# Two-byte one-hot selections with the entries of a batch innermost, widened by ScalarE, in a graph transformer layer

## The chip, the cores and the metric

The kernel runs on one core of a Trainium2 chip. The metric is the device time of one execution in microseconds (us). Three runs of the kernel before took 1121.39, 1125.89 and 1126.09 us; the median is 1125.89 us. A profile of one further execution gives spans, waits and the clock granted to TensorE.

The engines are named as in the profile: PE (TensorE, matmuls) and PEld (its weight loads), DVE (VectorE), ACT (ScalarE), POOL (GpSimd), SP (SyncE, which here issues DMAs). Each runs its own instructions in order.

## The reference, cut to what matters

A layer over 3125 nodes with 256 features: layer norm; a sparse graph network (`_L0_gnn_ref`); linear attention without a softmax (`_L0_mix_ref`); then a mixture of eight experts (`_L0_ffn_ref`). There are 53,125 edges, sorted by `dst`.

```python
xn = _layernorm(x)
# graph network: row = src, col = dst, val = edge_weight
spmm = lambda v: segment_sum(val[:, None] * v[col], row, num_segments=3125)
h = spmm(xn)
s0 = softmax(spmm(h) @ W0.T + b0)
s1 = softmax(spmm(concat([s0, s0])) @ W1.T + b1)      # the four heads are equal
x = x + tanh(concat([s0, s1]) + h) + mix(xn)          # mix: q, k, v; norms of k and v; (k^T v) / n
# experts: argmax of a gate, at most 489 tokens for an expert, two layers with relu
x = x + prob * expert(layernorm(x))
```

## The kernel before

The three sparse products are computed as dense ones. In a first stage the kernel builds the adjacency matrix (transposed, 3200 x 3200, fp32) in DRAM as `adj`; then it multiplies by it three times, in seven strips of up to 512 columns (`STRIPS`). The first strip of the first product and ten chunks (of 128 rows) of the second strip are already multiplied during the building. The keys and values of the attention (`kv_tile`, L728 on) are worked in beside the rest of the first product.

**The building (`from_runs`, L405 to L655).** Edges are sorted by target, so 625 groups of five targets (`GR`) each own a short run of edges. `search` finds the start of each run, `gather` (POOL, indirect DMA) fetches 128 edges for each of 125 groups, and `turn` splits source numbers into a block (one of 25) and a cell within the block (one of 128), and turns them on TensorE so that the 128 slots of a group lie on partitions. The result is `edge`: row in the group, block, cell and weight for each slot and group, in fp32. There are five such pieces of 125 groups.

A batch is 16 groups (`GB`); there are 39 full batches and one of a single group. `batch(b)` (L557) makes two matrices for each group on DVE: `lhs` (L564), 128 slots x (5 rows x 25 blocks), the product of "which row, times weight" (`in_row`) and "which block" (`in_blk`); and `rhs` (L569), 128 slots x 128 cells, the comparison of the numbers 0 to 127 with the slot's cell. Both are fp32 and hold 16 groups. `in_row` and `in_blk` come from `selections` (L539) for three batches at a time. One matmul for each group (L578; in fp32 two weight loads and two matmul instructions) sums the slots into 125 x 128 numbers in PSUM. Four groups fill a bank, ACT copies the bank to `st_rows` (L582), and SP writes the batch to `adj` (L589, L590). The four banks are two of `acc(1)` and two of `ps_b`; `st` has two buffers, `lhs` and `rhs` three each.

**The order of the work** is written out by hand in the loop at L618; nothing is planned by a scheduler (`tc.manual_schedule`). Every third batch a step of a node strip's layer norm is set between the batches. There are three steps: `norm_a` (DVE statistics L364, ACT square root L367) ahead of batches 0, 3, 6 ...; `norm_b` (DVE L373 and L375, four ACT instructions L379, eight TensorE transposes L386) behind batches 1, 4, 7 ...; `norm_c` (two ACT copies L393 out of PSUM) ahead of batches 2, 5, 8 ... Strips 2 to 6 are done so, which takes batches 0 to 14; strips 0 and 1 come before batch 0. `turn` stands ahead of a batch whose number leaves 1 when divided by 3, where a new piece is needed. `finish` (L325) prepares the gate's weights behind batch 18: two fp32 matmuls (L329) and a DVE instruction (L332) that waits for them.

`ask` loads a finished chunk of `adj` rows (L596, SP), and `take` multiplies it (L272: four instructions for a chunk, two feature halves in fp32). Reads go into `first_a`, six buffers.

After the building the pools of that stage are closed, new ones are laid in the same memory, and the weights of keys and values (`w_kv`, 512 KB) are loaded by POOL (L707); the first `kv_tile` (L731) needs them.

For the steps of the prediction: L564, L569, L549 (`in_blk`) and L544/L553 (`in_row`) are DVE; L582, L379, L393 and L367 are ACT; L578, L386, L329, L272 and L731 are TensorE.

Of the kernel before, what the change touches and what calls it, by code (L numbers as in the profile page):

```python
# [16 lines left out]
P = 128  # L17
# [47 lines left out]
def gps_layer(ctx: ExitStack, tc: tile.TileContext, a: dict, out: bass.AP):  # L65
# [211 lines left out]
    def load_constants():  # L277
# [47 lines left out]
        def finish():  # L325

            pm = mm()
            for d in range(2):
                nc.tensor.matmul(  # L329
                    pm[:, :NEXP], ones, gate_w[:, d, :], start=(d == 0), stop=(d == 1)  # L330
                )
            nc.vector.scalar_tensor_tensor(  # L332
# [4 lines left out]
        return finish  # L337
# [6 lines left out]
    def layer(net, runs):  # L344
# [25 lines left out]
        def norm_b(s):  # L370
# [7 lines left out]
            for j in range(nt):  # L378
# [3 lines left out]
                )  # L382
            mid[s] = [mm() for d in range(2)]
# [6 lines left out]
        def norm_c(s):  # L390
# [7 lines left out]
        xnT = xt_pool.tile([P, 2, NP], FP)  # L398

# [4 lines left out]
        def from_runs():  # L404
# [29 lines left out]
            nc.vector.tensor_copy(steps_f, si)  # L434
            ones_f = find.tile([P, EK], FP)
# [33 lines left out]
            edge = build.tile([P, 4, NG], FP)  # L469
# [18 lines left out]
            def turn(c, q, ends):  # L488
# [14 lines left out]
                for i in range(4):  # L503
                    nc.tensor.transpose(
                        pt[:, i * GC : (i + 1) * GC], q[:, i, :], ident[:GC, :GC]
                    )
                nc.scalar.copy(
                    edge[:, :, c * GC : (c + 1) * GC],
                    pt[:, : 4 * GC].rearrange("p (i g) -> p i g", g=GC),
                )  # L510
# [15 lines left out]
            norm_b(0)  # L526
            norm_a(1)
            norm_c(0)
            norm_b(1)
            norm_c(1)  # L530

            sel = ph.enter_context(tc.tile_pool(name="sel", bufs=3))
            pre = ph.enter_context(tc.tile_pool(name="pre", bufs=2))
            stage = ph.enter_context(tc.tile_pool(name="stage", bufs=2))
            first_a = ph.enter_context(tc.tile_pool(name="first_a", bufs=6))
            ps_0 = [acc(0) for _ in range(2)]
            some = {}

            def selections(g0):  # L539

                ng = min(3 * GB, NG - g0)
                row, blk, _, val = (edge[:, i, g0 : g0 + ng, None] for i in range(4))
# [5 lines left out]
                in_blk = pre.tile([P, 3 * GB, CA], FP, tag="in_blk", name="in_blk")[:, :ng]  # L548
                nc.vector.tensor_tensor(  # L549
                    in_blk, steps_f[:, None, :CA].to_broadcast([P, ng, CA]),  # L550
                    blk.to_broadcast([P, ng, CA]), ALU.is_equal,
                )
                nc.vector.tensor_tensor(in_row, in_row, val.to_broadcast([P, ng, GR]), ALU.mult)  # L553
                return in_row, in_blk

            def batch(b):
                g0 = b * GB  # L557
                ng = min(GB, NG - g0)
                if b % 3 == 0:
                    some[0] = selections(g0)  # L560
                o = b % 3 * GB
                in_row, in_blk = (x[:, o : o + ng] for x in some[0])
                lhs = sel.tile([P, GB, GR, CA], FP, tag="lhs", name="lhs")[:, :ng]
                nc.vector.tensor_tensor(  # L564
                    lhs, in_row[:, :, :, None].to_broadcast([P, ng, GR, CA]),
                    in_blk[:, :, None, :].to_broadcast([P, ng, GR, CA]), ALU.mult,
                )
                rhs = sel.tile([P, GB, P], FP, tag="rhs", name="rhs")[:, :ng]
                nc.vector.tensor_tensor(  # L569
                    rhs, steps_f[:, None, :].to_broadcast([P, ng, P]),  # L570
                    edge[:, 2, g0 : g0 + ng, None].to_broadcast([P, ng, P]), ALU.is_equal,
                )
                st = stage.tile([P, GB, P], FP, tag="st", name="st_rows")
                for j0 in range(0, ng, 4):
# [10 lines left out]
                    )  # L585
                rows = adj[g0 * GP * P : (g0 + ng) * GP * P, :].rearrange(
# [21 lines left out]
            last = NG // GB  # L608
# [9 lines left out]
            for b in range(last + 1):  # L618
                c = (min(NG, (b + 5) * GB) - 1) // GC
                s = 2 + b // 3  # L620
                more = s < len(STRIPS)
                if b % 3 == 0 and more:
                    norm_a(s)
                if b % 3 == 1 and c not in turned_c:
# [3 lines left out]
                if b % 3 == 2 and more:  # L628
                    norm_c(s)
# [642 lines left out]
```

## Time and profile before

| | us |
|---|---|
| median of three runs | 1125.89 |
| the profiled execution, its own time | 1125.04 |
| its span (first to last instruction) | 1122.8 |
| from the start to the first `lhs` | 28.4 |
| batches, first `lhs` to the last eviction | 28.4 to about 250.5 |
| rest of the chunks multiplied during building | 250.5 to 276.5 |
| everything behind it | 276.5 to 1122.8 |

| busy us in these stretches | PE | DVE | ACT |
|---|---|---|---|
| 0 to 28.4 | 13.30 | 19.22 | 9.03 |
| 28.4 to 250.5 | 192.84 | 207.46 | 107.39 |
| 250.5 to 276.5 | 22.70 | 0.87 | 0.22 |
| 276.5 to 1122.8 | 790.83 | 313.84 | 148.75 |

How to read it: the page of a profile gives the busy time of each engine, also as one digit (tenths) for each of 40 equal slices of the span. "PEclk" is the clock granted to TensorE, in tenths of full speed; its mean here is 0.959. A line of the groups names the source line, engine, operation, output and inputs, their shapes, the count, and then busy us, the mean ns of one, and the idle time of the engine just before them with what ended it ("<-DVE rhs L569" is a wait for that instruction). In the order in time a line begins with its start and its us, and successive instructions of one kind are merged ("x8"). Matmuls are pipelined, so their mean duration is longer than the distance between two of them.

### The profile page before, as it was taken

Reading aid. Unit: us, or ns where it says so; the run is one execution under the profiler, and the core shown is the slowest. Engines: PE = TensorE matmul, PEld = TensorE weight load, DVE = VectorE, ACT = ScalarE, POOL = GpSimd, SP = SyncE. Lnnn points to the kernel's source line nnn. Section 1 sums busy time; section 2 is a strip of 40 time slices with the busy share of each in tenths; the row PEclk is TensorE's granted clock in tenths of the full one; section 3 lists DMA queues with packets and bytes.
Section 4 is the critical chain, followed back from the end, with each engine's and each line's share of the span. In section 5 each row is a group of like instructions: output and inputs, shape, how many; then the busy total and the mean of one; then the engine's idle time right before and its main releaser. Section 6 shows DMA issues by size and latency. Waiting matters only on the chain. (4 is left out here: it accounts for less than half of the span.)

```text
span 1122.8 us, 11654 instructions
## 1 busy us (share of the span) xinstructions
PE 1019.7 (91%) x4305; PEld 666.5 (59%) x4305; DVE 541.4 (48%) x1123; ACT 265.4 (24%) x550; POOL 80.3 (7%) x92
## 2 busy tenths in 40 slices
PE   4679989988999999999999999998898955999995
PEld 2668777764444444455855544644454554888884
DVE  6999899960233434345614312222233350444444
ACT  3455534440000001011101011211112221333331
POOL 4102000001000000000000000001111120111111
PEclk7899989999999999999999999998998976999998
DMA  5476868784734237921566697788877726766630
GB/s 155 118 213 199 240 183 240 223 244 134 264 118 130 99 125 202 272 89 51 181 218 202 213 348 231 244 302 267 262 212 213 225 87 211 231 206 205 212 120 17
DMA packets 184982, 216.24 MB, mean 193 GB/s; under 512 B 9696, under 2 KB 127357, under 8 KB 184913
## 3 DMA queue, kind: packets, MB, share of 16 engines
q1 hardware_dynamic: 155339, 167.15, 47.8%
q10 hardware_dynamic: 22502, 29.99, 8.5%
q0 software_dynamic: 7072, 18.23, 5.8%
q8 instruction: 37, 0.61, 0.2%
q14 instruction: 32, 0.26, 0.1%
HBM read 156.06 MB, written 60.72 MB: 193 GB/s over the span
## 5 line engine op out<-in xcount | busy, mean ns | idle before, releaser
L272 PE MATMUL acc<-at,xn 128*128 128x512 f32 (+4 forms) x560 | 211.8, 526 | 0.0
L272 PEld LDWEIGHTS acc<-at,xn 128*128 128x128 f32 (+1 forms) x560 | 100.4, 190 | 91.7 <-issue 81.0
L272 PE MATMUL acc<-at,late 128*128 128x512 f32 (+4 forms) x350 | 144.5, 562 | 0.3 <-DMA at<-adj 0.3
L272 PE MATMUL acc<-at,g 128*128 128x512 f32 (+4 forms) x350 | 137.5, 541 | 0.0
L578 PE MATMUL acc<-rhs,lhs 128*125 128x128 f32 x626 | 85.7, 281 | 23.4 <-DVE rhs L569 14.1
L578 PEld LDWEIGHTS acc<-rhs,lhs 128*125 128x125 f32 x626 | 79.4, 195 | 35.7 <-issue 28.7
L272 PEld LDWEIGHTS acc<-at,late 128*128 128x128 f32 (+1 forms) x350 | 64.3, 197 | 60.6 <-issue 55.0
L272 PEld LDWEIGHTS acc<-at,g 128*128 128x128 f32 (+1 forms) x350 | 62.9, 190 | 59.4 <-issue 53.3
L569 DVE TENSOR_TENSOR rhs<-steps_f,edge 128x2048 f32<-128x2048 f32 (+1 forms) x40 | 89.4, 2234 | 0.0
L564 DVE TENSOR_TENSOR lhs<-in_row,in_blk 128x2000 f32<-128x2000 f32 (+1 forms) x40 | 87.5, 2188 | 1.3
L1127 PE MATMUL acc<-xeT,w 128*128 128x256 f32 (+1 forms) x384 | 86.7, 381 | 0.8 <-ACT xeT L1117 0.8
L1141 PE MATMUL mm<-w,hm 128*128 128x256 f32 (+1 forms) x384 | 84.9, 379 | 0.0
L578 PE MATMUL b<-rhs,lhs 128*125 128x128 f32 x624 | 83.5, 278 | 0.0
L1127 PEld LDWEIGHTS acc<-xeT,w 128*128 128x128 f32 x384 | 73.9, 195 | 9.2 <-ACT xeT L1117 1.2
L1141 PEld LDWEIGHTS mm<-w,hm 128*128 128x128 f32 (+1 forms) x384 | 71.6, 187 | 10.8
L578 PEld LDWEIGHTS b<-rhs,lhs 128*125 128x125 f32 x624 | 76.9, 193 | 0.0
L272 PE MATMUL acc<-a,xn 128*128 128x512 f32 (+1 forms) x140 | 64.0, 594 | 3.4 <-DMA a<-adj 3.4
L582 ACT COPY st_rows<-acc 125x512 f32<-125x512 f32 (+1 forms) x79 | 45.9, 581 | 88.5 <-PE acc L578 77.9
L737 DVE TENSOR_REDUCE kmean<-mm 128x8 f32<-128x512 f32 x25 | 17.3, 691 | 97.8 <-PE mm L731 97.8
L744 ACT ACTIVATE sq<-kv 128x512 f32<-128x512 f32 x25 | 15.7, 630 | 181.4 <-DVE kv L740 170.9
L731 PE MATMUL mm<-w_kv,xnT 128*128 128x512 f32 x100 | 49.1, 617 | 3.5 <-DMA w_kv<-in_wkv 3.5
L1147 DVE TENSOR_TENSOR y<-mm,b_e 128x256 f32<-128x256 f32 (+1 forms) x24 | 10.1, 421 | 85.9 <-PE mm L1141 80.5
(205 smaller groups left out, 958.3 us busy)
## 6 DMA issues: line engine op xcount, KB each, us to landing
at<-adj SPq DMA_DIRECT2D x54, 1280.0 KB
adj<-st_rows SPq DMA_DIRECT2D x39, 896.0 KB
w<-in_f_w ACTq DMA_DIRECT2D x24, 1024.0 KB
at<-adj SPq DMA_DIRECT2D x14, 1024.0 KB
at<-adj SPq DMA_DIRECT2D x12, 960.0 KB
a<-adj SPq DMA_DIRECT2D x34, 256.0 KB
xbuf<-empty POOLq DMA_DIRECT2D x1, 7710.0 KB, 45.5
at<-adj SPq DMA_DIRECT2D x12, 452.5 KB
```

The lines of the kernel that those rows point to most:

```text
L272: nc.tensor.matmul(ps[d][:, :w], stationary(c, d)[:k], a_rows[:k, :w], start=(c == 0), stop=(c == NT - 1),)
L564: nc.vector.tensor_tensor(lhs, in_row[:, :, :, None].to_broadcast([P, ng, GR, CA]), in_blk[:, :, None, :].to_broadcast([P, ng, GR, CA]), A ...
L569: nc.vector.tensor_tensor(rhs, steps_f[:, None, :].to_broadcast([P, ng, P]), edge[:, 2, g0 : g0 + ng, None].to_broadcast([P, ng, P]), ALU. ...
L578: nc.tensor.matmul(p[:GP, j * P : (j + 1) * P], lhs[:, j0 + j], rhs[:, j0 + j], start=True, stop=True,)
L582: nc.scalar.copy(st[:GP, j0 : j0 + nj, :], p[:GP, : nj * P].rearrange("p (g b) -> p g b", b=P),)
L731: nc.tensor.matmul(pkv, xnT[:, d, t * P : (t + 1) * P], w_kv[:, d, :], start=(d == 0), stop=(d == 1),)
L737: nc.vector.tensor_reduce(mean, p3, AX.X, ALU.add)
L744: nc.scalar.activation(sq, kv, AF.Square, scale=0.125)
L1127: nc.tensor.matmul(p[:, :slots], w1[:, d, f * P : (f + 1) * P], xeT[:, d, :slots], start=(d == 0), stop=(d == 1),)
L1141: nc.tensor.matmul(p[:n, :D], hm[:, f, c : c + n], w2[:, f, :], start=(f == 0), stop=(f == FC - 1),)
L1147: nc.vector.tensor_tensor(y, p[:n, :D], b2_e[:n], ALU.add)
```

## The change

`rhs` is no longer made in fp32 by DVE. `steps_w` (the numbers 0 to 127, each 16 times, bf16) is made once by ACT. DVE's `prepare` compares it with the cell numbers of a batch, now kept in bf16 (`edge_h`), into `cells`, bf16, laid out as cell by entry, the 16 entries innermost. ACT's `widen` copies `cells` into `rhs`, fp32, laid out as entry by cell as before; it reads across the entries, 32 bytes from one element to the next. `in_blk` is made in the same manner in bf16, entries innermost, and `lhs` reads it across the entries. Batch `b` issues `prepare(b + 1)` on DVE ahead of its matmuls, and `widen(b + 1)` behind its first eviction on ACT. The first selections cover one batch, the second two, and then three.

The transposes of `norm_b` become a step of their own (`norm_c`), and the copies `norm_d`; the steps now stand at batches 1, 2, 3 and behind 3, and so on. `finish` is a generator: its matmuls are issued at batch 20, its DVE instruction at 22. `w_kv` gets memory of its own and is loaded by POOL at batch 24. `first_a` has eight buffers. `turn` copies in two parts, into `edge_h` and `edge`.

```diff
--- before.py
+++ after.py
@@ -329,12 +329,13 @@
                 nc.tensor.matmul(
                     pm[:, :NEXP], ones, gate_w[:, d, :], start=(d == 0), stop=(d == 1)
                 )
+            yield
             nc.vector.scalar_tensor_tensor(
                 gate_c, pm[:, None, :NEXP].to_broadcast([P, 2, NEXP]), -1.0 / D, gate_w,
                 op0=ALU.mult, op1=ALU.add,
             )
 
-        return finish
+        return finish()
 
     def network(runs):
 
@@ -380,6 +381,9 @@
                     xn[:, t0 + j, :], xa[:, t0 + j, :], AF.Identity, bias=nmr[:, j : j + 1],
                     scale=rs[:, j : j + 1],
                 )
+
+        def norm_c(s):
+            t0, nt = STRIPS[s]
             mid[s] = [mm() for d in range(2)]
             for d, pt in enumerate(mid[s]):
                 for j in range(nt):
@@ -387,7 +391,7 @@
                         pt[:, j * P : (j + 1) * P], xn[:, t0 + j, d * P : (d + 1) * P], ident
                     )
 
-        def norm_c(s):
+        def norm_d(s):
             t0, nt = STRIPS[s]
             for d, pt in enumerate(mid.pop(s)):
                 nc.scalar.copy(xnT[:, d, t0 * P : (t0 + nt) * P], pt[:, : nt * P])
@@ -396,6 +400,10 @@
         att_scope = net.enter_context(ExitStack())
         xt_pool = att_scope.enter_context(tc.tile_pool(name="xt_pool", bufs=1, side="right"))
         xnT = xt_pool.tile([P, 2, NP], FP)
+        w_kv = xt_pool.tile([P, 2, 2 * D], FP)
+
+        def load_w_kv():
+            nc.gpsimd.dma_start(w_kv, a["wkv"].rearrange("(c p) n -> p c n", p=P))
 
 
 
@@ -432,6 +440,8 @@
             nc.vector.tensor_copy(g_thr, gi)
             steps_f = build.tile([P, P], FP)
             nc.vector.tensor_copy(steps_f, si)
+            steps_w = build.tile([P, P, GB], BF)
+            nc.scalar.copy(steps_w, steps_f[:, :, None].to_broadcast([P, P, GB]))
             ones_f = find.tile([P, EK], FP)
             nc.vector.memset(ones_f, 1.0)
             nc.vector.tensor_copy(tab[:, EK + 1 :], fi[:EL])
@@ -466,7 +476,8 @@
                 a[x].rearrange("p (k one) -> (p k) one", one=1) for x in ("src", "dst")
             )
             weights = a["edge_weight"].rearrange("(e one) -> e one", one=1)
-            edge = build.tile([P, 4, NG], FP)
+            edge = build.tile([P, 2, NG], FP)
+            edge_h = build.tile([P, 2, NG], BF)
             matched = build.tile([GC, NC], FP)
 
             def gather(c):
@@ -500,14 +511,15 @@
                 )
                 nc.vector.tensor_copy(q[:, 1:3, :], cut)
                 pt = mm()
-                for i in range(4):
+                for i, of in enumerate((1, 2, 0, 3)):
                     nc.tensor.transpose(
-                        pt[:, i * GC : (i + 1) * GC], q[:, i, :], ident[:GC, :GC]
-                    )
-                nc.scalar.copy(
-                    edge[:, :, c * GC : (c + 1) * GC],
-                    pt[:, : 4 * GC].rearrange("p (i g) -> p i g", g=GC),
-                )
+                        pt[:, i * GC : (i + 1) * GC], q[:, of, :], ident[:GC, :GC]
+                    )
+                for i, dst in enumerate((edge_h, edge)):
+                    nc.scalar.copy(
+                        dst[:, :, c * GC : (c + 1) * GC],
+                        pt[:, 2 * i * GC : (2 * i + 2) * GC].rearrange("p (i g) -> p i g", g=GC),
+                    )
                 hit = prep.tile([GC, SLOT], FP, tag="hit", name="hit")
                 nc.vector.tensor_scalar(hit, q[:, 0, :], float(GR) - 0.5, None, op0=ALU.is_lt)
                 nc.vector.scalar_tensor_tensor(
@@ -524,52 +536,81 @@
                     norm_a(0)
             early.close()
             norm_b(0)
+            norm_c(0)
             norm_a(1)
-            norm_c(0)
+            norm_d(0)
             norm_b(1)
             norm_c(1)
+            norm_d(1)
 
             sel = ph.enter_context(tc.tile_pool(name="sel", bufs=3))
             pre = ph.enter_context(tc.tile_pool(name="pre", bufs=2))
+            wide = ph.enter_context(tc.tile_pool(name="wide", bufs=2))
             stage = ph.enter_context(tc.tile_pool(name="stage", bufs=2))
-            first_a = ph.enter_context(tc.tile_pool(name="first_a", bufs=6))
+            first_a = ph.enter_context(tc.tile_pool(name="first_a", bufs=8))
             ps_0 = [acc(0) for _ in range(2)]
-            some = {}
-
-            def selections(g0):
-
-                ng = min(3 * GB, NG - g0)
-                row, blk, _, val = (edge[:, i, g0 : g0 + ng, None] for i in range(4))
+            some, made = {}, {}
+            last = NG // GB
+
+            def selections(b, nb):
+
+                g0 = b * GB
+                ng = min(nb * GB, NG - g0)
+                row, val = (edge[:, i, g0 : g0 + ng, None] for i in range(2))
                 in_row = pre.tile([P, 3 * GB, GR], FP, tag="in_row", name="in_row")[:, :ng]
                 nc.vector.tensor_tensor(
                     in_row, steps_f[:, None, :GR].to_broadcast([P, ng, GR]),
                     row.to_broadcast([P, ng, GR]), ALU.is_equal,
                 )
-                in_blk = pre.tile([P, 3 * GB, CA], FP, tag="in_blk", name="in_blk")[:, :ng]
+                in_blk = pre.tile([P, 3, CA, GB], BF, tag="in_blk", name="in_blk")
+                if ng < GB:
+                    nb, n = 1, ng
+                else:
+                    n = GB
                 nc.vector.tensor_tensor(
-                    in_blk, steps_f[:, None, :CA].to_broadcast([P, ng, CA]),
-                    blk.to_broadcast([P, ng, CA]), ALU.is_equal,
+                    in_blk[:, :nb, :, :n], steps_w[:, None, :CA, :n].to_broadcast([P, nb, CA, n]),
+                    edge_h[:, 0, g0 : g0 + ng].rearrange("p (b g) -> p b g", g=n)[
+                        :, :, None, :
+                    ].to_broadcast([P, nb, CA, n]),
+                    ALU.is_equal,
                 )
                 nc.vector.tensor_tensor(in_row, in_row, val.to_broadcast([P, ng, GR]), ALU.mult)
-                return in_row, in_blk
+                for i in range(nb):
+                    some[b + i] = in_row[:, i * GB : min((i + 1) * GB, ng)], in_blk[:, i]
+
+            def prepare(b):
+
+                g0 = b * GB
+                ng = min(GB, NG - g0)
+                cells = wide.tile([P, P, GB], BF, tag="cells", name="cells")[:, :, :ng]
+                nc.vector.tensor_tensor(
+                    cells, steps_w[:, :, :ng],
+                    edge_h[:, 1, None, g0 : g0 + ng].to_broadcast([P, P, ng]), ALU.is_equal,
+                )
+                if b not in some:
+                    selections(b, {0: 1, 1: 2}.get(b, 3) if b < last else 1)
+                in_row, in_blk = some.pop(b)
+                lhs = sel.tile([P, GB, GR, CA], FP, tag="lhs", name="lhs")[:, :ng]
+                nc.vector.tensor_tensor(
+                    lhs, in_row[:, :, :, None].to_broadcast([P, ng, GR, CA]),
+                    in_blk[:, :, :ng].rearrange("p b g -> p g b")[:, :, None, :].to_broadcast(
+                        [P, ng, GR, CA]
+                    ),
+                    ALU.mult,
+                )
+                made[b] = lhs, cells
+
+            def widen(b):
+                lhs, cells = made[b]
+                ng = cells.shape[2]
+                rhs = sel.tile([P, GB, P], FP, tag="rhs", name="rhs")[:, :ng]
+                nc.scalar.copy(rhs, cells.rearrange("p c g -> p g c"))
+                made[b] = lhs, rhs
 
             def batch(b):
                 g0 = b * GB
                 ng = min(GB, NG - g0)
-                if b % 3 == 0:
-                    some[0] = selections(g0)
-                o = b % 3 * GB
-                in_row, in_blk = (x[:, o : o + ng] for x in some[0])
-                lhs = sel.tile([P, GB, GR, CA], FP, tag="lhs", name="lhs")[:, :ng]
-                nc.vector.tensor_tensor(
-                    lhs, in_row[:, :, :, None].to_broadcast([P, ng, GR, CA]),
-                    in_blk[:, :, None, :].to_broadcast([P, ng, GR, CA]), ALU.mult,
-                )
-                rhs = sel.tile([P, GB, P], FP, tag="rhs", name="rhs")[:, :ng]
-                nc.vector.tensor_tensor(
-                    rhs, steps_f[:, None, :].to_broadcast([P, ng, P]),
-                    edge[:, 2, g0 : g0 + ng, None].to_broadcast([P, ng, P]), ALU.is_equal,
-                )
+                lhs, rhs = made.pop(b)
                 st = stage.tile([P, GB, P], FP, tag="st", name="st_rows")
                 for j0 in range(0, ng, 4):
                     nj = min(4, ng - j0)
@@ -583,6 +624,8 @@
                         st[:GP, j0 : j0 + nj, :],
                         p[:GP, : nj * P].rearrange("p (g b) -> p g b", b=P),
                     )
+                    if j0 == 0 and b < last:
+                        widen(b + 1)
                 rows = adj[g0 * GP * P : (g0 + ng) * GP * P, :].rearrange(
                     "(g p b) one -> p g (b one)", p=GP, b=P
                 )
@@ -605,7 +648,8 @@
             todo[NT - 3 : NT - 3] = [(1, c) for c in range(AHEAD)]
             ready = []
             sums = {0: ps_0}
-            last = NG // GB
+            prepare(0)
+            widen(0)
 
             def ask():
                 s, c = todo.pop(0)
@@ -617,21 +661,27 @@
 
             for b in range(last + 1):
                 c = (min(NG, (b + 5) * GB) - 1) // GC
-                s = 2 + b // 3
-                more = s < len(STRIPS)
-                if b % 3 == 0 and more:
-                    norm_a(s)
-                if b % 3 == 1 and c not in turned_c:
-                    turn(c, *fetched[c])
-                    if c + 2 < NC:
-                        fetched.append(gather(c + 2))
-                if b % 3 == 2 and more:
+                s, step = 2 + (b - 1) // 3, b % 3
+                if step == 1:
+                    if s < len(STRIPS):
+                        norm_a(s)
+                    if c not in turned_c:
+                        turn(c, *fetched[c])
+                        if c + 2 < NC:
+                            fetched.append(gather(c + 2))
+                if step == 2 and s < len(STRIPS):
+                    norm_b(s)
+                if step == 0 and 0 < b and s < len(STRIPS):
                     norm_c(s)
+                if b in (20, 22):
+                    next(finish, None)
+                if b == 24:
+                    load_w_kv()
+                if b < last:
+                    prepare(b + 1)
                 batch(b)
-                if b % 3 == 1 and more:
-                    norm_b(s)
-                if b == 18:
-                    finish()
+                if step == 0 and 0 < b and s < len(STRIPS):
+                    norm_d(s)
                 while todo[0][0] == 0 and (todo[0][1] + 1) * P <= (b - 1) * GB * GR:
                     ask()
                 if todo[0][0] == 1 and b > last - 2:
...
@@ -697,14 +749,12 @@
         g_pool = att_scope.enter_context(tc.tile_pool(name="g_pool", bufs=1, side="right"))
         g = g_pool.tile([P, NT, HD], FP)
         att = att_scope.enter_context(tc.tile_pool(name="att", bufs=1, side="right"))
-        w_kv = att.tile([P, 2, 2 * D], FP)
         w_q = att.tile([P, 2, D], FP)
         w_o = att.tile([P, 2, D], FP)
         b_o = att.tile([P, D], FP)
         kvT = att.tile([P, 2, P], FP)
         kvo = att.tile([P, 2, D], FP)
         w_mix = att.tile([P, 2, D], FP)
-        nc.gpsimd.dma_start(w_kv, a["wkv"].rearrange("(c p) n -> p c n", p=P))
         nc.gpsimd.dma_start(w_q, a["wq"].rearrange("(c p) n -> p c n", p=P))
         nc.gpsimd.dma_start(w_o, a["woT"].rearrange("(c p) n -> p c n", p=P))
         nc.gpsimd.dma_start(b_o, rows_all(a["bo"], 0, D))
```

More of the change, by code (lines that the diff above doesn't have):

```diff
@@ L662, in layer @@
             general()
+            load_w_kv()
             load_x()
@@ L667, in layer @@
                 norm_c(s)
+                norm_d(s)
         gnn = net.enter_context(ExitStack())
```

## The prediction

> **What bounds the kernel now.** I read the page first, to find the stretch that the change touches, then the busy time by stage, then the groups of instructions of that stretch by shape, and last the order in time around its stalls. The page's slices (28.1 us each) show the stretch.
>
> ```profile
> PE 1019.7 (91%) x4305; PEld 666.5 (59%) x4305; DVE 541.4 (48%) x1123; ACT 265.4 (24%) x550; POOL 80.3 (7%) x92
> PE   4679989988999999999999999998898955999995
> DVE  6999899960233434345614312222233350444444
> ACT  3455534440000001011101011211112221333331
> ```
>
> Slices 2 to 9 are the building of the adjacency matrix: only there is DVE full, and ACT half free. Behind 276 us TensorE is the bound and, but for the key weights, the change does nothing there. A group of three batches, from one `lhs` to the third after it, is the unit. Columns: stretch, its us, then PE, PEld, DVE, ACT and POOL busy.
>
> ```profile
> 45.99:64.75 18.76, 14.32 (x121) 13.20 (x121) 18.45 (x26) 11.66 (x22) 5.21 (x3) 1.00 0.72 207
> 64.75:81.83 17.08, 12.80 (x97) 10.92 (x96) 16.84 (x18) 9.16 (x19) 0.00 (x0) 0.99 0.64 188
> 115.00:130.22 15.22, 15.22 (x108) 12.57 (x107) 15.11 (x10) 7.43 (x14) 0.00 (x0) 1.00 0.76 222
> 130.22:151.67 21.45, 16.34 (x111) 14.60 (x110) 16.38 (x17) 7.30 (x13) 0.00 (x0) 0.84 0.58 171
> 166.88:182.09 15.21, 14.21 (x107) 12.14 (x106) 15.11 (x9) 7.03 (x12) 0.00 (x0) 1.00 0.81 238
> ```
>
> DVE sets the pace: 17.1 us for a group with norms, 15.2 us without, 1.2 to 1.7 more where a chunk is turned. TensorE stands close behind. ACT has 7 to 9 us of work in 15 to 17. The groups between 28 and 252 us give the prices (busy us, mean ns of one):
>
> ```profile
> L569 DVE TENSOR_TENSOR rhs<-steps_f,edge 128x2048 f32<-128x2048 f32 x39 | 89.1, 2284 | 0.0
> L564 DVE TENSOR_TENSOR lhs<-in_row,in_blk 128x2000 f32<-128x2000 f32 x39 | 87.2, 2237 | 1.2
> L549 DVE TENSOR_TENSOR in_blk<-steps_f,edge 128x1200 f32<-128x1200 f32 x13 | 18.2, 1401 | 0.0
> L582 ACT COPY st_rows<-b 125x512 f32<-125x512 f32 x78 | 45.7, 585 | 23.2 <-PE b L578 22.8 <-issue 0.3
> L582 ACT COPY st_rows<-acc 125x128 f32<-125x128 f32 x1 | 0.3, 265 | 3.1 <-PE acc L578 3.1
> ...
> L379 ACT ACTIVATE xn<-xa,nmr,rs 128x256 f32<-128x256 f32 x17 | 8.9, 592 | 0.0
> ```
>
> The order in time shows TensorE's cadence and three stalls:
>
> ```profile
> 139.66 0.17 DVE L332 SCALAR_TENSOR_TENSOR gate_c<-mm,gate_w 128x16 f32<-128x16 f32 x1 [5.00 <-PE mm L329]
> ...
> 145.48 2.04 PE L578 MATMUL acc<-rhs,lhs 128*125 128x128 f32 x8 [4.37 <-DVE rhs L569]
> ...
> 157.27 1.04 PE L578 MATMUL b<-rhs,lhs 128*125 128x128 f32 x8
> 158.14 1.04 PE L578 MATMUL acc<-rhs,lhs 128*125 128x128 f32 x8
> ...
> 159.89 1.88 PE L272 MATMUL acc<-a,xn 128*128 128x512 f32 x4
> 161.61 1.04 PE L578 MATMUL acc<-rhs,lhs 128*125 128x128 f32 x8
> ...
> 282.57 5.37 PE L731 MATMUL mm<-w_kv,xnT 128*128 128x512 f32 x8 [3.52 <-DMA w_kv<-in_wkv]
> ```
>
> A quarter of a batch takes 0.87 us (157.27 to 158.14), a batch 3.49; a chunk of the first product 1.72 (159.89 to 161.61), and a group of 240 rows brings 1.875 chunks. So TensorE needs 3 x 3.49 + 1.875 x 1.72 = 13.7 us for a group. In the DMA view of 160 to 220 us, 242 GB/s take 82.6% of the engines, so 293 are full; a group moves 3 x 1.024 MB out and 1.875 x 0.262 MB in, 3.56 MB, 12.2 us. These are the floors under any faster DVE.
>
> **The change, part by part.** *Cells in bf16.* `rhs` (2284 ns) becomes `cells`, all operands 2 bytes, 16 entries innermost. Nearest row: L569 itself, 2048 elements at 1.04 ns plus 0.15 us. By that row at worst nothing is saved. [...] I take 1.22 us: 1.06 saved in a batch, 3.2 in a group.
>
> *Blocks in bf16.* [...] `in_row` stays fp32.
>
> *`lhs`.* It is still 2000 fp32 products, but `in_blk` is now read with 32 bytes from one 2-byte element to the next. Every long DVE row here reads adjacent or repeated elements: L564 gives 2.24 us and is the lower end. [...] No row here tells. [...] I take 3.6: +1.36 a batch, +4.1 a group, more than the 3.8 of cells and blocks. DVE then stands at 15.2 - 3.8 + 4.1 = 15.5 without norms and 17.4 with them: no faster than now. By the row it would stand at 11.4 and 13.3.
>
> *Widening on ACT.* New: 39 copies of 2048 elements from `cells`, again 32 bytes apart. ACT's L582 takes 265 ns for 128 elements and 585 for 512: 0.833 ns an element and 158 ns fixed. By this row, though it reads adjacent elements, a copy costs 1.87 us. [...] I take 3.7.
>
> ACT's sum for a group: 12 evictions at 0.50 when back to back (two L393 copies together are 1.08 us, one is 0.585), 6.0; three widenings at 3.6 (less the same 0.09 overlap), 10.8; in the norm stage four L379 (2.07 together), two L393 (1.08), one L367 (0.30), 3.45. That is 16.8 without norms and 20.3 with. ACT executes in order: behind each `widen` stand the other three evictions of its batch, and TensorE waits for those banks, SP for the rows they finish. So ACT, not DVE (15.5, 17.4), sets the pace.
>
> *Norms in four steps.* The transposes leave the spot where TensorE waited for L379 (7.8 us in all by their row); the DVE and ACT work is the same. With TensorE no bound, zero; worth up to 7.8 us if it becomes one.
>
> *Gate bias in two steps, at batches 20 and 22.* DVE's 5.0 us wait goes; its matmuls have two batches to finish. Under an ACT bound this is no gain of its own.
>
> *Key weights.* The transfer moves to POOL at batch 24. POOL's gathers have ended by then (no POOL work after 120 us), so nothing queues behind it; 512 KB are 1.8 us of DMA time beside queues that are 80% busy. TensorE's 3.52 us go; the L731 after it also ran cold (5.37 us for 8, against 3.4 at the cadence of L272). Next late is the load of strip 1, issued at 277.2 us and not delayed. Gain 3.5, between 1 and 5.
>
> *Small things.* `steps_w` is one 1.87 us ACT copy near 12 us, where ACT had waited 12.3 us and `xn` waits until 17.3 for DVE: hidden; uncovered 1.9. Two edge copies for one: 250 elements are 366 ns, so +0.15 for each of 5 turns. Eight buffers instead of six: no time, since TensorE waited only about 4 us for rows. The first selections cover one batch, and the widening runs beside `lhs`: the first `lhs` is done at about 31.8 us by my prices (26.2, where the first selection starts, and 1.2 + 0.8 + 3.6), so the first matmul comes 1.1 before today's 32.9.
>
> **The sum.** Before, first to last eviction: 35.0 to 250.5 us. After, ACT from 33.9: five norm groups, 5 x 20.3 less 2.1 for the two short strips plus 1.5 for two turns, 101; eight without, 8 x 16.8 + 1.5, 136. Last eviction at 33.9 + 237 = 271, 20.5 later. The tail of the first product (250 to 276 us) is TensorE's and only shifts. Less 3.5 for the key weights: +17; I add 1 for waits between ACT and DVE, which are close. The profiled execution took 1125.04 us (span 1122.8), 0.85 under the median 1125.89: 1125.9 + 18 = 1144.
>
> **The rivals.** (A) A hop costs nothing. DVE 11.4 and 13.3; ACT 6.0 + 5.3 = 11.3, with norms 14.8; TensorE 13.7, with transposes 14.6. Groups fall to about 15.5 with norms and 14.0 without: 5 x 15.5 + 8 x 14.0 + 2 = 191.5 against the 214.0 from batch 0 to 39 now. That is -22.5, start -2, weights -3.5, and +4 for the two `st` buffers, each held through eviction and landing while DMA is near full: 1102. For it: L582's slope, and nothing in the trace that is slow. [...] 30%.
>
> [...] 17%.
>
> (C) The forecast, 1144, its own range 1134 to 1160. 38%. If `cells` doesn't get the double rate, DVE needs 18.7 and 20.5 and the end is near 1160; I count that here.
>
> [...] 15%.
>
> The decision lies in one mechanism, the price of a 32-byte hop: with `lhs` at 3.6 the end goes above today's once a widening passes about 3 us (1.39 ns an element), since ACT's norm groups (9.45 + 3 x 2.91 = 18.2) then outlast DVE's.
>
> **Chances.** 0.5% (5.6 us) is about what a measurement of this kernel tells from no change. Faster: A and under half of B, 0.37. Same: the rest of B, 0.11. Slower: C and D, 0.52. For 8 in 10 the range runs from 1098, under A, to 1180, into D.
>
> **What would show it.** A `cells` row near 1.22 us; `lhs` at 3.6 (2.24 refutes); the widening at 3.7 (1.87 gives A); ACT above 9 tenths in slices 2 to 9 with DVE waiting for ACT's reads; TensorE waiting for ACT. No L332 or w_kv wait. A wait of ACT on landings of `st_rows` would mean that DMA is the new bound, as in A.

## The result, and the profile after

The changed kernel takes 1164.53 us (median of four runs, 1161.39 to 1166.9) against 1125.47 (four runs, one more than the three above) for the kernel before: a ratio of 1.0353, 95% interval 1.0318 to 1.0388. It is slower, as forecast, but by 39 us where 18 were forecast. The profiled execution took 1164.01 us, its span is 1161.9.

The slices of the page (29.0 us each) show which engine is full now:

```profile
PE 1033.3 (89%) x4305; PEld 677.1 (58%) x4305; DVE 561.1 (48%) x1126; ACT 405.5 (35%) x597; POOL 77.9 (7%) x92
PE   4677788888989999999999999999888973999995
DVE  5999898984033344444543332123332350444444
ACT  4899999997000000001101001012221231333331
```

ACT stands at 8 in slice 2 and at 9 in slices 3 to 9, where it was half free. DVE is at 8 and 9 and no longer full: it was busy 68.86 of the 80 us from 200 to 280, where before a group without norms was busy 15.11 of 15.21. The groups of the building, from 28 to 300 us (busy us, mean ns of one, idle time before it and what ended it):

```profile
L607 ACT CAST rhs<-cells 128x2048 f32<-128x2048 bf16 x39 | 155.1, 3978 | 1.7 <-issue 1.2 <-DVE cells L586 0.5
L594 DVE TENSOR_TENSOR lhs<-in_row,in_blk 128x2000 f32<-128x2000 f32 x39 | 148.8, 3815 | 1.3
L619 PE MATMUL acc<-rhs,lhs 128*125 128x128 f32 x626 | 94.7, 299 | 48.4 <-ACT rhs L607 45.1 <-DVE nmr L376 3.0
...
L586 DVE TENSOR_TENSOR cells<-steps_w,edge_h 128x2048 bf16<-128x2048 bf16 x39 | 52.7, 1352 | 12.9 <-ACT rhs L607 8.7 <-ACT edge_h L519 4.1
```

TensorE's row of the kernel before:

```profile
L578 PE MATMUL acc<-rhs,lhs 128*125 128x128 f32 x626 | 85.7, 281 | 23.4 <-DVE rhs L569 14.1 <-issue 7.3 <-DVE rs L373 1.3
```

The widening costs 3.98 us (forecast 3.7), `lhs` 3.82 in place of 2.24 (3.6), `cells` 1.35 (1.22). TensorE, which had waited 14.1 us for DVE's `rhs`, now waits 45.1 us for ACT's. ACT's own order in time shows a batch:

```profile
202.83 3.96 ACT L607 CAST rhs<-cells 128x2048 f32<-128x2048 bf16 x1
206.71 0.57 ACT L623 COPY st_rows<-b 125x512 f32<-125x512 f32 x1
207.18 0.58 ACT L623 COPY st_rows<-acc 125x512 f32<-125x512 f32 x1
207.66 0.59 ACT L623 COPY st_rows<-b 125x512 f32<-125x512 f32 x1
208.14 0.60 ACT L623 COPY st_rows<-acc 125x512 f32<-125x512 f32 x1
208.62 3.97 ACT L607 CAST rhs<-cells 128x2048 f32<-128x2048 bf16 x1
```

From widening to widening it is 5.8 us without a gap: 3.9 for the widening, then four evictions (copies out of PSUM) that start 0.48 apart. A batch before, paced by DVE, took 5.07.

The last eviction begins at 290.8 us (250.45 before), the building's last matmul (the count of edges) at 317.7 (276.5), and from there to the end of the span it is 844.2 us (846.3). So +40.4, +0.8 and -2.1 make the 39.1 us between the spans.

### The profile page after: what moved, and what is told of

Same layout as the page of the kernel before. It is cut to its first block, busy times and chain, and to the rows that moved or that the text cites. A ratio compares the mean times of both kernels' runs of the same rounds, so it can differ in the third digit from the quotient of the medians.

```text
span 1161.9 us, 11707 instructions
## 1 busy us (share of the span) xinstructions
PE 1033.3 (89%) x4305; PEld 677.1 (58%) x4305; DVE 561.1 (48%) x1126; ACT 405.5 (35%) x597; POOL 77.9 (7%) x92
## 5 line engine op out<-in xcount | busy, mean ns | idle before, releaser
L607 ACT CAST rhs<-cells 128x2048 f32<-128x2048 bf16 (+1 forms) x40 | 155.6, 3889 | 1.7 <-issue 1.2
L594 DVE TENSOR_TENSOR lhs<-in_row,in_blk 128x2000 f32<-128x2000 f32 (+1 forms) x40 | 149.2, 3729 | 1.4
L619 PE MATMUL acc<-rhs,lhs 128*125 128x128 f32 x626 | 94.7, 299 | 48.4 <-ACT rhs L607 45.1
L619 PEld LDWEIGHTS acc<-rhs,lhs 128*125 128x125 f32 x626 | 84.8, 209 | 64.0 <-ACT rhs L607 61.8
L619 PE MATMUL b<-rhs,lhs 128*125 128x128 f32 x624 | 88.6, 289 | 0.0
L619 PEld LDWEIGHTS b<-rhs,lhs 128*125 128x125 f32 x624 | 82.4, 205 | 0.0
L586 DVE TENSOR_TENSOR cells<-steps_w,edge_h 128x2048 bf16<-128x2048 bf16 (+1 forms) x40 | 53.5, 1336 | 13.8 <-ACT rhs L607 9.6
L623 ACT COPY st_rows<-acc 125x512 f32<-125x512 f32 (+1 forms) x79 | 49.2, 623 | 16.2 <-PE acc L619 11.2
L1181 ACT ACTIVATE hm<-acc,b_e 128x256 f32<-128x256 f32 (+1 forms) x96 | 44.1, 467 | 30.2 <-PE acc L1177 29.2
```

What stands on the lines that cost most here:

```text
L586: nc.vector.tensor_tensor(cells, steps_w[:, :, :ng], edge_h[:, 1, None, g0 : g0 + ng].to_broadcast([P, P, ng]), ALU.is_equal,)
L594: nc.vector.tensor_tensor(lhs, in_row[:, :, :, None].to_broadcast([P, ng, GR, CA]), in_blk[:, :, :ng].rearrange("p b g -> p g b")[:, :, No ...
L607: nc.scalar.copy(rhs, cells.rearrange("p c g -> p g c"))
L619: nc.tensor.matmul(p[:GP, j * P : (j + 1) * P], lhs[:, j0 + j], rhs[:, j0 + j], start=True, stop=True,)
L623: nc.scalar.copy(st[:GP, j0 : j0 + nj, :], p[:GP, : nj * P].rearrange("p (g b) -> p g b", b=P),)
L1181: nc.scalar.activation(hm[:, f, :slots], p[:, :slots], AF.Relu, bias=b1_e[:, f : f + 1], scale=1.0)
```

## The experiments

Three theories stood at first. The forecast's: the 32-byte step from element to element (the prediction's "hop") is what makes ACT's widening and DVE's `lhs` dear, and ACT's full queue is the bound. Its rivals: what is dear is the cast from 2 bytes, or the two engines' work on one memory; or it is the new order of work. All ratios are to the kernel before, run beside the kernel in question, with the 95% interval behind. The edits are shortened to the lines that matter.

**The step, one operand at a time (e1, e2, e3).** In e1 the 16 entries of a batch are laid as eight pairs, so that a reader steps 4 bytes; `lhs` becomes two instructions.

```diff
-cells = wide.tile([P, P, GB], BF)                    # cell, entry
+cells = wide.tile([P, GB // 2, P, 2], BF)            # pair, cell, entry of the pair
-nc.scalar.copy(rhs, cells.rearrange("p c g -> p g c"))
+nc.scalar.copy(rhs.rearrange("p (q g) c -> p q g c", g=2), cells.rearrange("p q c g -> p q g c"))
-nc.vector.tensor_tensor(lhs, in_row.., in_blk (step 32 bytes).., ALU.mult)
+for e in range(2): nc.vector.tensor_tensor(lhs[:, e::2], in_row[:, e::2].., in_blk[:, :, :, e].., ALU.mult)
```

e2 does this for the cells alone, e3 for the blocks alone.

> The changed kernel with entries in pairs: cells and blocks are laid out as pair, cell, entry of the pair, so that a reader across the entries steps 4 bytes, from one word to the next, in place of 32; `lhs` is then two DVE instructions of 1000 elements. Same numbers, same order of work. Theory (the 32-byte step is the price): the widening falls from 3.98 us to about 1.87, `lhs` from 3.82 to two of about 1.15, `cells` stays at 1.35, ACT is no longer full, and the time falls below the kernel before: about 1103 us (1095 to 1112). Rival 1 (the widening is slow because it reads 2-byte elements or turns them into fp32, or because DVE works on the same memory): the widening stays near 3.9 us and the time near 1160. Rival 2 (any step between elements costs, 4 bytes too): widening 3 us or more, time above 1130.

> Only the cells in pairs; blocks stay with 16 entries innermost. Theory: widening 1.87 us, `lhs` still 3.8; DVE sets the pace with 1.35 + 3.8 + 0.5 us a batch, 17.5 us a group without norms... that is 3 x (1.27 + 3.74) + 1.5 = 16.5 and with norms 18.5: about 1130 us (1122 to 1142). Rival (ACT's work alone counted): about 1105.

> Only the blocks in pairs; cells stay with 16 entries innermost. Theory: `lhs` 2.3 us in two instructions, widening still 3.98; ACT stays full and the time falls little: about 1161 us (1154 to 1165). Rival (DVE's slower `lhs` is what lengthened the stage): about 1125.

Measured: e1 1122.5 us, ratio 0.9975 (0.9962 to 0.9988); e2 1177.15, 1.0455 (1.0425 to 1.0485); e3 1163.19, 1.0339 (1.0297 to 1.0382). The groups of e1:

```profile
L619 DVE TENSOR_TENSOR lhs<-in_row,in_blk 128x1000 f32<-128x1000 f32 x78 | 89.9, 1194 | 1.3
...
L593 DVE TENSOR_TENSOR cells<-steps_c,edge_h 128x2048 bf16<-128x2048 bf16 x39 | 89.0, 2282 | 8.1 <-ACT edge_h L523 8.1
...
L629 ACT CAST rhs<-cells 128x2048 f32<-128x2048 bf16 x39 | 74.2, 1903 | 11.7 <-DVE cells L593 9.3 <-issue 2.1
```

The same cast of the same 2-byte elements takes 1.90 us in place of 3.98: the step was the price, and the rival of the cast falls. `lhs` is back at its old rate (1.04 ns an element). e2 and e3 take the two readers apart:

```profile
L629 ACT CAST rhs<-cells 128x2048 f32<-128x2048 bf16 x39 | 74.1, 1901 | 14.3 <-DVE cells L593 12.0 <-issue 2.1
```

```profile
L629 ACT CAST rhs<-cells 128x2048 f32<-128x2048 bf16 x39 | 154.8, 3969 | 1.2 <-issue 1.2
```

In e2 DVE still steps 32 bytes and the widening is cheap; in e3 DVE steps 4 and the widening is dear. So ACT's price is that of ACT's own step, and the rival of the shared memory falls too. e3 also shows which of the two held the end: with `lhs` cheap again and the widening dear, nothing is won.

But e1 missed its 1103 us, and e2 its 1130 by 47, in the main by the same term: `cells` went from 1.35 to 2.28 us, though its operands were still of 2 bytes (0.93 us in each of 39 batches is 36 us of DVE, which bounds e2). That became a question of its own.

**The rest of the change alone (e4).** `rhs` and `lhs` in fp32 on DVE as before, no widening; all else as in the changed kernel.

```diff
-cells = ...; widen(b + 1) behind the first eviction
+nc.vector.tensor_tensor(rhs, steps_f.., edge[:, 2, ..].., ALU.is_equal)     # in prepare(b)
```

> The rest of the change alone: `rhs`, `lhs` and their inputs in fp32 on DVE as before, no widening; four-step norms, one batch of preparation ahead, gate bias at batches 20 and 22, key weights at batch 24, eight row buffers stay. Theory: DVE is the bound as before, without its 5 us wait for the gate's matmuls: about 1116 us (1111 to 1121). Rival (the new order of work is itself part of the loss): above 1127.

Measured 1121.1 us, 0.9969 (0.9956 to 0.9982), at the upper end of the expected range. The order of work is no part of the loss; the whole loss is in bf16 and widening.

**How the step is priced, and what slows `cells` (e5, e6, e7).** The same kernel with entries in fours (8 bytes) and eights (16 bytes); e7 has fours for the cells alone, with blocks in fp32; only the cell numbers are then in `edge_h`. For the step they ask where between 4 and 32 bytes the price sets in.

```diff
-CI, BI = 2, 2
+CI, BI = 4, 4        # e5;   8, 8 in e6;   CI = 4 and fp32 blocks in e7
```

> Entries in fours for cells and blocks, so that the step of the readers is 8 bytes; `lhs` is four DVE instructions of 500. In e1 `cells` went from 1.35 to 2.28 us though all its operands stayed 2 bytes wide: 1024 rows of two in place of 128 rows of sixteen. Theory for that (each innermost row costs one further cycle of 1.04 ns): 2048 / 2 + 512 rows give 1.6 + 0.15 = 1.75 us for `cells`. Rival (rows under some length lose the double rate as a whole): 2.28. [...]

> Entries in eights, step 16 bytes; `lhs` is two DVE instructions of 1000. Theory for `cells` (a cycle for each row): 1024 + 256 cycles, 1.48 us; rival 1.35 or 2.28. [...]

> Cells in fours, blocks and `lhs` in fp32 as in the kernel before (one `lhs` of 2.24 us, in_blk 1.40). If e5's step is free: DVE 3 x (1.67 + 2.16) + 2.1 = 13.6 us a group against 15.2 before, TensorE's 13.7 next, time about 1108 (1103 to 1116). If 8 bytes cost the full price: ACT full, about 1160.

Measured: e5 1117.63 us, 0.9925 (0.9908 to 0.9943); e6 1167.97, 1.0364 (1.0327 to 1.0401); e7 1116.25, 0.992 (0.9892 to 0.9948). e5 is quicker than the kernel before, and e6 about as slow as the changed kernel (1.0353); e7 came just above its range (1103 to 1116). First two lines of e5, then of e6, then one of e7:

```profile
L629 ACT CAST rhs<-cells 128x2048 f32<-128x2048 bf16 x39 | 81.5, 2091 | 3.5 <-DVE cells L593 1.9 <-issue 1.6
...
L593 DVE TENSOR_TENSOR cells<-steps_c,edge_h 128x2048 bf16<-128x2048 bf16 x39 | 68.2, 1750 | 14.2 <-ACT edge_h L523 14.2
```

```profile
L629 ACT CAST rhs<-cells 128x2048 f32<-128x2048 bf16 x39 | 153.8, 3943 | 3.5 <-DVE cells L593 2.1 <-issue 1.3
L619 DVE TENSOR_TENSOR lhs<-in_row,in_blk 128x1000 f32<-128x1000 f32 x78 | 151.7, 1989 | 1.3
```

```profile
L583 DVE TENSOR_TENSOR cells<-steps_c,edge_h 128x2048 bf16<-128x2048 bf16 x38 | 46.3, 1219 | 16.7 <-ACT rhs L604 16.3
```

| step, bytes | widening, us | its ns an element | `lhs`, ns an element |
|---|---|---|---|
| 4 (e1) | 1.90 | 0.85 | 1.04 |
| 8 (e5) | 2.09 | 0.94 | 1.05 |
| 16 (e6) | 3.94 | 1.85 | 1.84 |
| 32 (after) | 3.98 | 1.87 | 1.83 |

(158 ns taken off a widening, 150 off an instruction of `lhs`.) The price sets in between 8 and 16 bytes and grows no more up to 32. What in the memory sets this price no run shows. At 32 bytes both engines pay nearly the same absolute price, 1.83 and 1.87 ns.

e7's `cells` at 1.22 us in fours, where e5 has 1.75, refutes the theory that each row costs a cycle. What differs is where the numbers begin.

**Half words (e9, e11).** In the changed kernel the cell numbers are the second row of `edge_h`, 625 entries of 2 bytes in, so they begin 1250 bytes in, in the middle of a 4-byte word. e9 is e7 in pairs, with the cell numbers at the head of their tile, as in e7; e11 is the changed kernel with one number changed.

```diff
-edge_h = build.tile([P, 2, NG], BF)
+edge_h = build.tile([P, 2, NG + 1], BF)      # e11: row 1 begins on a whole word
```

> Cells in pairs again (step 4 bytes), blocks and `lhs` in fp32 as in e7, and the bf16 cell numbers at the head of their tile. In e7 `cells` in fours took 1.22 us where e5's took 1.75. What differs is where the numbers begin: in e1 to e6 and in the changed kernel they are the second row of `edge_h`, 625 entries of 2 bytes in, so every read of a row begins on an odd entry. Theory: each innermost row that begins on half a word costs one further cycle; aligned, `cells` takes 1.22 us in pairs too. Then DVE 12.0 us a group, ACT 11.2, TensorE 13.7: about 1113 us (1109 to 1117). Rival (the number of rows costs, e7 is another thing): `cells` 2.28 us as in e1 and about 1121.

> The changed kernel with one number changed: rows of `edge_h` have 626 entries, so that the cell numbers begin on a whole word. Theory: `cells` falls from 1.35 to 1.22 us; nothing else, since ACT with its widening is full: 1164 us (1160 to 1167). Rival (DVE shares the bound): about 1159.

Measured: e9 1110.38 us, 0.9872 (0.9854 to 0.9889), `cells` 1.22 us in pairs; e11 1161.31, 1.0327 (1.0308 to 1.0346), `cells` 1.22. First e9, then e11:

```profile
L583 DVE TENSOR_TENSOR cells<-steps_c,edge_h 128x2048 bf16<-128x2048 bf16 x38 | 46.3, 1220 | 18.8 <-ACT rhs L604 18.3 <-ACT edge_h L520 0.5
```

```profile
L586 DVE TENSOR_TENSOR cells<-steps_w,edge_h 128x2048 bf16<-128x2048 bf16 x38 | 46.3, 1218 | 11.2 <-ACT rhs L607 10.9 <-ACT edge_h L519 0.2
```

So an innermost row that begins on half a word costs about as much as one element of the fp32 comparison (1.04 ns): 128, 256, 512 and 1024 rows (the changed kernel, e6, e5, e1) cost 133, 268, 531 and 1063 ns over 1219, which is 1.04 to 1.05 each. In the changed kernel this matters little, since ACT is the bound: the intervals of e11 and the changed kernel overlap.

**Where the improved versions stop (e10, e13, e14, e15).** ACT in e9 waits for landings of `st_rows`:

```profile
L623 ACT COPY st_rows<-acc 125x512 f32<-125x512 f32 x78 | 46.3, 593 | 37.7 <-DMA adj<-st_rows 29.7 <-PE acc L619 5.8 <-issue 2.2
```

```diff
-stage = tile_pool(name="stage", bufs=2);  first_a = tile_pool(name="first_a", bufs=8)
+stage = tile_pool(name="stage", bufs=3);  first_a = tile_pool(name="first_a", bufs=5)
```

e10 is e9 so changed, e13 the changed kernel, e14 the kernel before (from six row buffers); e15 is e9 with five row buffers alone. A third `st` with all eight row buffers was not run.

> e9 with three `st` buffers, and five row buffers, since the memory gives no more. In e5 and e7 ACT waited 21 to 22 us for landings of `st_rows`. Theory: those waits are the two buffers; with three they go and TensorE's own work is left: about 5 us less than e9. Rival (DMA is full, the wait moves to the rows that TensorE needs): the same as e9, or slower.

> The changed kernel with three `st` buffers and five row buffers. Theory (the stage is ACT's own work; of ACT's 18 us without work only 2.5 were waits for landings): within 5 us of 1164 in the building; behind it the stage of strip 1 may start earlier, as in e10 (10 us): 1150 to 1164. Rival (waits for the buffers are what lengthened the stage over the forecast): the last eviction more than 10 us earlier than 290.8.

> The kernel before with three `st` buffers and five row buffers. Theory: DVE is its bound in the building (one wait of 2.2 us for a landing in all), so the building keeps its length; only the earlier start of strip 1's rows can gain: 1114 to 1124. Rival (e10's gain over e9 lies in the buffers whatever else is done): about 1106.

> e9 with five row buffers in place of eight and still two `st` buffers: which part of e10's 18.6 us is the memory that five leave. Theory: the waits for landings (29.7 us of ACT in e9) stay, the rows of strip 1 come earlier: about 1102. Rival (all of it is the third `st`): 1110.

Measured: e10 1091.73 us, 0.9713 (0.9696 to 0.973); e13 1158.77, 1.0294 (1.0266 to 1.0323); e14 1127.65, 1.0012 (1.0001 to 1.0023); e15 1113.69, 0.9886 (0.9854 to 0.9918). e10 gained far more than the 5 us expected, e13 fell in its range; e14 (1114 to 1124) and e15 (1102) did not gain what was expected of an earlier start of strip 1. The third buffer helped only where the engines had become quicker than two buffers turn round: not before (e14), little in the changed kernel (last eviction 285.9 in place of 290.8), 18.6 us in e9. In e10 TensorE is the bound at last, with DMA close behind (130 to 222 us; PE, PEld, DVE, ACT and POOL busy, granted clock, DMA share, GB/s):

```profile
130.00:222.00 92.00, 90.60 (x668) 77.23 (x666) 71.28 (x63) 73.27 (x101) 0.00 (x0) 1.00 0.92 253
```

The spans of the two profiled executions are 22.7 us apart (1109.2 and 1086.5): 12.8 lie in the building, 9.9 behind it. There TensorE no longer waits for strip 1's rows (3.80 us in e9), and its next 20 matmuls take 8.75 us in place of 11.78, at a granted clock of 1.00 in place of 0.74. e15 shows that five row buffers alone don't do that, and e13 that the two changes of buffers don't do it in every kernel. The traces name a cause: POOL's loads of three other weights (`w_q`, `w_o`, `b_o`). First e9, then e10:

```profile
263.40 0.75 POOL L758 DMA_DIRECT2D w_q<-in_wq  x1 [160.50 <-PE mm L699]
```

```profile
228.80 0.75 POOL L758 DMA_DIRECT2D w_q<-in_wq  x1 [126.82 <-DMA a<-adj]
```

In e9 they go out together with strip 1's rows (issued at 263.57) and share the DMA engines with them (25.3% of the engines' time from 263 to 274 us); TensorE can start on the rows 10.1 us after their issue. In e10 they go out 22 us ahead of the rows, since `w_q` waits there for another transfer than in e9 before its memory is free, and the rows were ready within 6.1 us. In every other kernel that loads the key weights early (the changed one, e1 to e9, e11, e13, e15) the three loads go out with the rows, and TensorE waits 2.6 to 4.6 us. No run moved these loads alone, so this cause is read from the traces and not tested.

**The two small parts alone (e8, e12).** Into the kernel before: the key weights at batch 24 (e8), the gate in two steps at 20 and 22 (e12).

> The kernel before with one part alone: the key weights loaded at batch 24. The prediction's 3.5 us: about 1121. What the changed kernel's trace suggests (the stretch from the end of the first product's tail to the end of the span is 2.1 us shorter, since strip 1's rows are then waited for): about 1122.5. Rival (the transfer delays the building): no gain, 1124 or more.

> The kernel before with one part alone: the gate's matmuls at batch 20, its DVE instruction at batch 22. Theory: DVE's wait of 5.0 us goes, and DVE sets the pace there: about 1120.5 us. Rival (TensorE was behind at that place, and DVE's wait was paid by TensorE's lag): between 1123 and 1126.

Measured: e8 1125.71 us, 1.0003 (0.999 to 1.0015); e12 1120.77, 0.9968 (0.9955 to 0.9981). In e8 the wait of 3.52 us is gone, and TensorE stands before strip 1's rows instead, whose first 20 matmuls then take 10.46 us, where they took 8.82 before (granted clock 0.84 from 286.3 to 297 us, 1.00 before from 287.8 to 296.5):

```profile
286.31 9.18 PE L272 MATMUL acc<-at,xn 128*128 128x512 f32 x17 [3.00 <-DMA at<-adj]
```

## Why the prediction was right in kind and short in size

**Right.** ACT became the bound, through the step of 32 bytes, and DVE gained nothing. No run on record when the prediction was written shows its 1.22 us for `cells`, its 0.6 us a group for blocks, its 3.6 us for `lhs` or its 3.7 for the widening. In their place the runs showed `cells` at 1.35 us in the changed kernel and 1.22 with rows that begin on whole words (e11), against 2.28 for the fp32 `rhs`; `in_blk` at 0.78 us in place of 1.40, the 0.6 a group; `lhs` at 3.82 us, 1.83 ns an element; and the widening at 3.98, 1.87 ns an element. The "wait of ACT on landings" came in the quick kernels (22.5 us in e5, 29.7 in e9), but it did not mean, as the prediction has it, that DMA is the bound: e10's third buffer took it away while the DMA engines carried more (253 GB/s in the stretch above, 238 in e9 from 130 to 235 us).

**The step that failed: the sum of ACT's time, above all its term for waits.** From first to last eviction 237 us were forecast, with 1 added behind for waits, and 255.7 came (35.1 to 290.8). The parts, from the trace, each instruction counted from its start to the next start less the wait between:

| ACT, us | forecast | measured |
|---|---|---|
| 39 widenings | 140.4 | 38 at 3.84 and a short one, 146.2 |
| evictions | 78 | 156 at 0.50, 77.6 |
| norms and turns | 18.2 | 16.2 |
| without work | 1 (added behind) | 15.6 |

So the waits made 14.6 us more than forecast, and the dearer step 5.8. The prediction put it thus: "I add 1 for waits between ACT and DVE, which are close". Of the 15.6 us only 0.7 were waits for DVE. The others were for TensorE and for landings:

```profile
ACT st_rows L623 <- PE acc L619: 11.2, 6, 5.9
ACT st_rows L623 <- DMA adj<-st_rows: 2.5, 6, 1.1
```

(Of the 11.2 us, 2.6 lie ahead of the first eviction, outside the 255.7; the 18 us in the expectation of e13 count them too.) The longest, 5.9 us, is the lone last group: its matmul stands in TensorE's queue behind two chunks, and the rows of the second must first land (TensorE waits 2.60 for them). Before, the last eviction waited 3.07 at this place. Most of the other waits for TensorE come where a chunk, a turn's transposes or the gate's matmuls stand ahead of a quarter of a batch. So ACT, "the bound" by its sum, was still without work for 15.6 of 255.7 us, for the most part where TensorE, which feeds it, stood behind something else. e13 bears this out in part: with the waits for landings gone, ACT is 11.9 us without work, and the last eviction comes 4.9 us earlier (0.4 of it from an earlier first one). What would remove the rest was not tested.

**The second term: "Gain 3.5, between 1 and 5" for the key weights.** e8 shows none in the kernel before: strip 1's rows, which the prediction named as next and "not delayed", were late at once (3.00 us). The matmuls of which the prediction says that they "ran cold" took 5.37 us for 8 at a granted clock of 0.69 (282.5 to 288 us, before), and 3.93 for 8 in the changed kernel. There TensorE's first matmul of these rows waits 3.27 us, and the stretch behind the building is 2.1 us shorter.

**The start.** "The first matmul comes 1.1 before today's": it came at 33.05 against 32.93. The prediction put `steps_w` at nothing ("hidden; uncovered 1.9"). It wasn't hidden: a second table load of 1.28 us stands with the copy:

```profile
13.16 1.28 ACT L444 ACT_TABLE_LOAD   x1 [13.16 <-DVE st L365]
14.45 1.90 ACT L444 CAST steps_w<-steps_f 128x2048 bf16<-128x2048 f32 x1
16.37 1.28 ACT L368 ACT_TABLE_LOAD   x1
```

Before, one such load of 1.28 us stands there, at 12.33 us. Now the square root comes at 17.66 us, and the first `xn` at 18.40 in place of 17.30. The delay of 1.1 us runs on to ACT's copy of `edge_h`, for which DVE waits until 27.20, and the first `lhs` begins at 29.17, where the prediction has 28.2.

Together: 14.6 for waits, 5.8 for the step, 1.2 for the start, 1.4 for the weights and 0.8 for the tail, less 2.4 for evictions, norms and turns, are 21.4 us, and make up the 21 between 18 and 39.

**The gate.** "No gain of its own" under ACT's bound can't be read off the changed kernel alone; in the kernel before it is worth 4.0 us (e12) of its 5.0 us of DVE wait.

**Rival A** said that the step costs nothing, and was wrong in that. Of a kernel without the price it was near: e9, with `lhs` in fp32, takes 1110 and e10, without the brake of two `st` buffers that A named, 1092, on either side of A's 1102. Rivals B (17%) and D (15%) rest on other prices of the step, which no run shows: measured at 32 bytes were 1.83 ns an element on DVE and 1.87 on ACT. Small slips among the prediction's chances (0.11 and 0.52 for 0.10 and 0.53) change nothing.

## What to carry to other kernels

Here DVE's bf16 comparison took 1.22 us in place of 2.28 (e11), and whoever read such a result at a step of 16 or 32 bytes paid for it: ACT 1.85 to 1.87 ns an element, DVE 1.83 to 1.84. At 4 and 8 bytes (pairs and fours) ACT took 0.85 to 0.94 and DVE 1.04 to 1.05. So keep the reader's step at 8 bytes or less, as e5 and e9 did, and let rows of 2-byte operands begin on whole words: each row on half a word cost DVE 1.04 ns. Before work is moved to an idle engine, add up its sum, and then look at what it will stand behind (15.6 us without work here, where 1 was added for waits); and when the engines become quicker, count the buffers through which the results leave (18.6 us from e9 to e10). Taking away one wait was worth nothing where the next transfer was due: in e8 a wait of 3.52 us gave way to one of 3.00. And a small instruction added to an engine ahead of the first batch is not free because the engine is idle there: look at what it brings with it (here 1.28 us of table load beside a copy of 1.90) and what stands behind it.

## What the runs showed of the hardware that had not been expected

- ACT and DVE were both slower at the longer steps, for 4, 8, 16 and 32 bytes: ACT's widening 0.85, 0.94, 1.85 and 1.87 ns an element, DVE's `lhs` 1.04, 1.05, 1.84 and 1.83.
- A 2-byte operand whose innermost rows begin on half a word cost DVE 1.04 ns more for each such row: the 1219 ns of `cells` became 1352, 1487, 1750 and 2282 with 128, 256, 512 and 1024 rows. With 1024 rows the gain over fp32 was gone (2284 ns).
- With rows of only two elements `cells` still took 1.22 us (e9), as with rows of sixteen (e11).
- ACT's cast from bf16 to fp32 at a step of 4 bytes (1.90 us for 2048) cost what L582's fp32 copies lead to expect (1.87).
- A plain ACT copy ahead of the first square root brought a table load of its own: two of 1.28 us in the changed kernel's first 18 us, one in the kernel before.
